# A sparse attention layer: the second part's q is projected in natural row order and gathered from a DRAM table

## The chip, the cores and the metric

The kernel runs on one core of a Trainium2 chip. The metric is the device time of one execution in microseconds (us). The engines are PE (matmul), DVE (vector), ACT (scalar), POOL (GpSimd) and SP; each works through its own instructions in order, and they meet at semaphores. DMAs are issued from SP, ACT and POOL.

## The reference

One graph layer over 4096 nodes with 512 features, 8 heads of 64. `adj` is a symmetric 0/1 matrix with some 17 ones in a row, and a node attends to its neighbours alone. Masks are all ones here. Cut to what is computed:

```python
hs = layer_norm(x, ln1_scale, ln1_bias)
ht = layer_norm(h_target, ln1_scale, ln1_bias)
q = (ht @ Wq + bq).reshape(T, H, HD) / sqrt(HD)
k = (hs @ Wk + bk).reshape(S, H, HD)
v = (hs @ Wv + bv).reshape(S, H, HD)
logits = where(adj != 0, einsum('thd,shd->hts', q, k), NEG)
ctx = einsum('hts,shd->thd', softmax(logits), v).reshape(T, D)
ht = ht + ctx @ Wo + bo
ht = layer_norm(ht, ln2_scale, ln2_bias)
ff = gelu(ht @ W1) @ W2
out = layernorm(x + ht + ff)
```

## The kernel before

The kernel doesn't form the 4096 × 4096 logits. It makes lists of neighbours and gathers only their k and v rows.

**Projections and lists.** `project` norms x, projects k and v, and writes them as rows of 4 KB (k, then v) to the table `kvd` in DRAM. Beside it, `edges` reads the adjacency in quarters of 128 rows × 1024 columns (512 KB each), takes the sign on ACT (L729) with the row's degree as a by-product, and finds the set columns on DVE with MAX8 (L736, five to a quarter) and a few more instructions per tile (L743 to L760). Each row ends as a record: degree (DEG), row number (TGT), row number within its part (ROW), the mean and scale of its first norm (RST), and its neighbours (from E0). The rows are in two parts, 0 to 2047 and 2048 to 4095, of 16 tiles each. `sort` orders a part by degree and scatters its records to DRAM (`recs_d`), so that the rows of one tile have about as many neighbours each; the lists of tile i are CAPS_A or CAPS_B long. Part 0 is sorted before the attention begins; the rest of part 1's lists (`other_lists`) is made beside the attention of part 0.

**Attention.** `attention` goes through the 32 tiles in groups of two (the first and last group have one tile). For a tile, `prefetch` loads its records and `front` makes its q: it gathers the rows of `h_target` by TGT (256 KB), norms them on ACT (L999), turns them with four transposes (L1003), brings them out with scale and bias as four ACT instructions (L1006), projects q with four matmuls (L1012; two records each in the profile), and brings q out on DVE (L1017). The tile `tq` then holds q in its first half and the normed rows, transposed, in its second. L995 is a tie: it makes the norm wait for the newest logits (`latest`). The neighbours come in pieces of S = 3: a piece is three indirect DMAs from POOL (L967), 512 KB each, into a ring of 17 or 20 places; then k times q (L1220) and the sum over each head (L1225) on DVE, the exponential on ACT (L1229, L1238), v times p on DVE (L1184) and ACT (L1204), and on PE the sum over neighbours, as transposes that accumulate in the PSUM tile `cps` (L1192). In the second part DVE first adds two of the three neighbours (L1188).

`finish` ends a tile. It divides by the sum (L1104), puts the normed rows back into natural order with four transposes into the PSUM tile `pa` (L1112), adds ctx @ Wo to them there (L1116), copies the sum to `h` on ACT (L1121), and takes the statistics for the second norm on DVE (L697). A group's normed h goes, transposed, into `h2T`.

**FFN.** `feed` takes a group's `h2T` through W1 (L1325), gelu on ACT (L1328) and W2 (L1334). `end` adds x, norms, and scatters the rows to the output.

**Order.** The streams attention, FFN, `other_lists` and `weights` (late loads of half of W1 and W2) are generators, and `_weave` picks the one with the smallest sum of yielded costs; a group has UNIT = 60 of cost in the attention and as much in the FFN, and `other_lists` starts at WAIT = 40. This gives priorities; a scheduler with a model of its own then fixes each engine's order. Pools hand out buffers in turn by name: `tq` has three, `xt`, `gt`, `h2T` and the PSUM tiles `pf` and `t` have two each.

Of the kernel before, what the change touches and what calls it, by code (L numbers as in the profile page):

```python
# [8 lines left out]
F32 = mybir.dt.float32  # L9
I32 = mybir.dt.int32  # L10
U8 = mybir.dt.uint8
AF = mybir.ActivationFunctionType
ALU = mybir.AluOpType
AX = mybir.AxisListType
# [3 lines left out]
P = 128  # L18
# [425 lines left out]
def adj_resnorm_kernel(  # L444
# [33 lines left out]
    nc = tc.nc  # L478
# [35 lines left out]

    rest_d = dram.tile([N, 2 * SEG * 8], F32, name="rest_d")
# [17 lines left out]
    with tc.tile_pool(name="keep", bufs=1) as keep:  # L533
# [17 lines left out]
        with ExitStack() as late:  # L551
# [157 lines left out]
            def quarter(i, h):  # L709
                if i < RINGED:  # L710
                    a = ring[:, (i * NQ + h) % DEEP, :].bitcast(I32)
                else:
                    a = turn_of("wide", wide)
                nc.sync.dma_start(a, adj[i * P:(i + 1) * P, h * QW:(h + 1) * QW])
                return a

# [247 lines left out]
            recs, tqs, h2Ts, done, ready, latest, newest = {}, {}, {}, set(), [], [], []  # L964

            def gather(dst, table, idx):
                nc.gpsimd.indirect_dma_start(  # L967
                    out=dst, out_offset=None, in_=table[:, :],
                    in_offset=bass.IndirectOffsetOnAxis(ap=idx, axis=0))
# [13 lines left out]
            def front(i, idle=0):  # L983
# [3 lines left out]
                tq = sp.tile([P, 2 * D], F32, name="tq", bufs=3)  # L987
                t = tq[:, :D]
# [89 lines left out]
            def finish(i, p, cps, group, hs, mv):  # L1078
# [31 lines left out]

                for c in range(KC):
                    nc.tensor.matmul(pa[:, c * P:(c + 1) * P], tq[:, D + c * P:D + (c + 1) * P],  # L1112
                                     ident, is_transpose=True, start=c == 0, stop=False,
                                     skip_group_check=True)
                for c in range(KC):
                    nc.tensor.matmul(pa, ct[:, c, :], wo[:, c, :], start=False,  # L1116
                                     stop=c == KC - 1, skip_group_check=True)
# [3 lines left out]
                nc.scalar.copy(h, pa)  # L1121
# [45 lines left out]
            def attention():  # L1167
# [41 lines left out]
                for group in GROUPS:  # L1209
# [3 lines left out]
                    for i in group:  # L1213
                        cps = ps.tile([P, KC, P], F32, name="cps", bufs=2)
                        while k < len(SG) and SG[k][0] == i:
                            _, j0, n = SG[k]
                            while i not in tqs:
# [7 lines left out]
                            nc.vector.tensor_reduce(lg[:, :n, :],  # L1225
                                                    kv[:, :n, :D].rearrange("p j (h d) -> p j h d", h=H),
                                                    AX.X, ALU.add)
# [147 lines left out]

            def chain(gens):
                for g in gens:
                    yield from g
# [65 lines left out]
            def other_lists():  # L1444
                for cost in ed:
# [5 lines left out]
                   (weights(), 0))  # L1451
# [35 lines left out]
```

## Time and profile before

| | us |
|---|---|
| median of 3 runs | 1814.09 |
| lowest, highest | 1813.91, 1817.4 |
| the profiled execution | 1817.49 |
| its span in the profile | 1815.5 |
| first gather of k and v lands, first L1220 | 308.1 |
| first FFN matmul (L1325) | 373.5 |
| scatter of part 1's records (L854) | 627.1 to 664.7 |
| last tile's L1104 | 1706.5 |

The profile gives starts and durations of one execution. Busy times are the union of an engine's instructions. A release is what an idle engine was waiting for. A row of a stretch gives its limits, its length, and for each engine its busy time and number of instructions, then the granted PE clock, the share of the 16 DMA engines, and the GB/s moved.

### The profile page before, as it was taken

How to read it: one execution, taken by the hardware profiler on the slowest of the kernel's cores; microseconds unless marked ns; L12 is line 12 of the kernel's file. 1: busy time of each engine (PE TensorE's matmuls, PEld its weight loads, DVE VectorE, ACT ScalarE, POOL GpSimd, SP SyncE). 2: the span in 40 equal slices, each digit the busy share in tenths (PEclk: the TensorE clock that was granted, in tenths of full speed). 3: DMA queues.
4: the chain of work that ended last, by engine and by line, in shares of the span. 5: the costliest groups of instructions: out<-in, count | busy, mean ns of one | idle time of the engine just before them, and what ended most of it. 6: DMA issues, size and time to landing. Idle time of an engine off the chain costs nothing. (4 is left out here: it accounts for less than half of the span.)

```text
span 1815.5 us, 22973 instructions
## 1 busy us (share of the span) xinstructions
PE 1677.8 (92%) x7030; PEld 1097.9 (60%) x7030; DVE 1436.5 (79%) x2660; ACT 1224.1 (67%) x3121; POOL 982.2 (54%) x834
## 2 busy tenths in 40 slices
PE   7989984597999979999999989999999999999997
PEld 3434442465766656766776757666666666666664
DVE  6989876899999837777978989978878797988200
ACT  5767654487987736766778868877777676787311
POOL 1000144656566676766678788867575665763101
PEclk9999996698999989999999999999999999999998
DMA  9999968989887557777878878787776776774000
GB/s 344 366 380 372 344 198 319 404 287 332 271 305 256 201 173 243 258 255 267 273 263 302 293 260 295 249 285 250 241 266 222 248 251 238 244 248 153 18 6 26
DMA packets 140269, 463.26 MB, mean 255 GB/s; under 512 B 16500, under 2 KB 21672, under 8 KB 140136
## 3 DMA queue, kind: packets, MB, share of 16 engines
q0 software_dynamic: 96656, 342.64, 55.8%
q1 hardware_dynamic: 35664, 95.98, 15.0%
q10 hardware_dynamic: 7816, 23.08, 3.3%
q8 instruction: 58, 0.95, 0.2%
q14 instruction: 75, 0.61, 0.1%
HBM read 430.75 MB, written 30.89 MB: 254 GB/s over the span
## 5 line engine op out<-in xcount | busy, mean ns | idle before, releaser
L967 POOL DMA_INDIRECT kv<-kvd,rec x603 | 758.1, 1257 | 347.5 <-PE cps L1192 139.7
L1334 PE MATMUL po<-w,gt 128*128 128x512 f32 x1024 | 466.4, 598 | 16.2 <-ACT gt L1328 16.2
L1325 PE MATMUL pf<-h2T,w 128*128 128x256 f32 (+1 forms) x2176 | 465.9, 368 | 0.1
L1325 PEld LDWEIGHTS pf<-h2T,w 128*128 128x128 f32 x2176 | 389.3, 191 | 64.5 <-issue 20.3
L1220 DVE TENSOR_TENSOR kv<-kv,tq 128x1536 f32<-128x1536 f32 (+2 forms) x211 | 351.6, 1675 | 68.3 <-DMA kv<-kvd,rec 56.2
L1204 ACT ACTIVATE kv<-kv,pa 128x64 f32<-128x64 f32 x1520 | 391.0, 336 | 4.3
L1225 DVE TENSOR_REDUCE lg<-kv 128x24 f32<-128x1536 f32 (+2 forms) x211 | 350.1, 1666 | 1.4
L1334 PEld LDWEIGHTS po<-w,gt 128*128 128x128 f32 x1024 | 188.8, 192 | 212.4 <-issue 194.3
L1192 PEld LDWEIGHTS cps<-ident,kv 128*128 128x128 f32 x2008 | 240.2, 145 | 109.4 <-issue 59.2
L1192 PE MATMUL cps<-ident,kv 128*128 128x128 f32 x2008 | 264.5, 280 | 44.1 <-DVE kv L1184 24.5
L1184 DVE TENSOR_TENSOR kv<-kv,p 128x1024 f32<-128x1024 f32 (+1 forms) x211 | 251.0, 1193 | 22.8 <-ACT p L1229 20.3
L687 POOL TENSOR_TENSOR n_rs<-n_ve,mhalf 128x2 f32<-128x2 f32 (+2 forms) x51 | 50.8, 997 | 329.1 <-DVE n_ve L680 165.3
L729 ACT ACTIVATE kv<-kv 128x1024 uint8<-128x1024 int32 x128 | 134.9, 1056 | 100.0 <-DMA kv<-in_adj_dram 51.7
L1328 ACT ACTIVATE gt<-pf 128x512 f32<-128x512 f32 x128 | 76.4, 597 | 93.8 <-PE pf L1325 75.8
L1328 ACT ACT_TABLE_LOAD x104 | 133.4, 1283 | 1.7
L736 DVE MAX8 cand<-kv 128x8 uint16<-128x103 uint16 (+1 forms) x640 | 131.8, 252 | 0.8 <-DVE R L755 0.2
L930 PE MATMUL pq<-wk,h2T 128*128 128x512 f32 x256 | 120.8, 616 | 12.1 <-ACT tq L932 7.2
L1012 PE MATMUL t<-wq,tq 128*128 128x512 f32 x256 | 118.2, 605 | 5.6 <-ACT tq L1006 5.6
L930 PE MATMUL pq<-wv,h2T 128*128 128x512 f32 x256 | 115.5, 594 | 6.4 <-ACT kv L729 3.0
L1229 ACT ACTIVATE p<-lg 128x24 f32<-128x24 f32 (+2 forms) x179 | 39.2, 219 | 113.0 <-DVE lg L1225 88.8
L1116 PE MATMUL t<-wo,rb 128*128 128x512 f32 x256 | 115.2, 592 | 0.0
L930 PEld LDWEIGHTS pq<-wk,h2T 128*128 128x128 f32 x256 | 48.9, 197 | 69.9 <-issue 55.2
(160 smaller groups left out, 1582.2 us busy)
## 6 DMA issues: line engine op xcount, KB each, us to landing
kv<-in_adj_dram SPq DMA_DIRECT2D x128, 512.0 KB
kvd<-tq ACTq DMA_DIRECT2D x24, 512.0 KB
kv<-kvd,rec POOLq DMA_INDIRECT x603
kv<-in_L_gnn_h_target_dram SPq DMA_DIRECT2D x32, 256.0 KB
kv<-in_x_dram SPq DMA_DIRECT2D x15, 512.0 KB
rest_d<-gid SPq DMA_DIRECT2D x32, 160.0 KB
w<-in_L_gnn_W_dram SPq DMA_DIRECT2D x4, 1024.0 KB
kvd<-kv ACTq DMA_DIRECT2D x8, 512.0 KB
```

The costliest lines, as they stand in the source:

```text
L729: nc.scalar.activation(sg, a, AF.Sign, accum_out=dpart[:, i, h:h + 1])
L736: nc.vector.max(cand[:, h * SQ + s, :], wd[:, w0:w1])
L930: nc.tensor.matmul(pkv, hT[:, kc, j * P:(j + 1) * P], w[:, kc, :], start=kc == 0, stop=kc == KC - 1)
L967: nc.gpsimd.indirect_dma_start(out=dst, out_offset=None, in_=table[:, :], in_offset=bass.IndirectOffsetOnAxis(ap=idx, axis=0))
L1184: nc.vector.tensor_tensor(v4, v4, p[:, j0:j0 + m, :].unsqueeze(3) .to_broadcast([P, m, H, HD]), ALU.mult)
L1192: nc.tensor.matmul(cps[:, c, :], kv[:, j, D + c * P:D + (c + 1) * P], ident, is_transpose=True, start=j0 + j == 0 and c == 0, stop=j0 + n ...
L1204: newest[:] = [nc.scalar.mul(v, v, pa[:, hd:hd + 1]).ins]
L1220: nc.vector.tensor_tensor(kv[:, :n, :D], kv[:, :n, :D], tq[:, :D].unsqueeze(1).to_broadcast([P, n, D]), ALU.mult)
L1225: nc.vector.tensor_reduce(lg[:, :n, :], kv[:, :n, :D].rearrange("p j (h d) -> p j h d", h=H), AX.X, ALU.add)
L1325: nc.tensor.matmul(pf[:, k, :], w1[(f0 + k) // KC][:, kc, (f0 + k) % KC * P:((f0 + k) % KC + 1) * P], h2T[:, kc, :w], start=kc == 0, stop= ...
L1328: nc.scalar.activation(gt, pf, AF.Gelu_apprx_tanh)
L1334: nc.tensor.matmul(po[j], gt[:, k, j * P:(j + 1) * P], w2[(f0 + k) // KC][:, (f0 + k) % KC, :], start=False, stop=f0 + k == FC - 1, skip_g ...
```

## The change

Part 1's q no longer comes from `front`. A new stream `natural` goes through part 1's 16 tiles of `h_target` in the order of their rows: a load from SP, the norm with the moments that `Rs[1]` holds, four transposes, four ACT instructions with scale and bias, the q projection, four transposes back to natural order, and one row of 4 KB (q, then the normed rows) in the new DRAM table `qd`. It is woven in from the attention's start, at a cost of 5 to a tile. A tile of part 1 then gathers its 512 KB of rows from `qd` by ROW in one indirect DMA, and `finish` adds the normed rows on DVE in place of the transposes and of the ACT copy. Its copy of DEG and TGT to `tags` is issued after the newest logits. Part 0's tiles are as before.

```diff
+    qd = dram.tile([NBT * P, 2 * D], F32, name="qd")
...
+            def behind(ins):
+                return tc.issue_after(ins[-1]) if ins else nullcontext()
...
                 tq = sp.tile([P, 2 * D], F32, name="tq", bufs=3)
+                if TILES[i][0] >= PARTS[1][0] * P:
+                    gather(tq, qd, rec[:, ROW:ROW + 1])
+                    for _ in range(3 + idle):
+                        yield
+                    with behind(logits):
+                        nc.vector.tensor_copy(tags[:, i, :], rec[:, DEG:TGT + 1])
+                    tqs[i] = tq
+                    return
...
+                natural_q = TILES[i][0] >= PARTS[1][0] * P
+                if not natural_q:
+                    for c in range(KC):
+                        nc.tensor.matmul(pa[:, c * P:(c + 1) * P], tq[:, D + c * P:D + (c + 1) * P],
+                                         ident, is_transpose=True, start=c == 0, stop=False,
+                                         skip_group_check=True)
                 for c in range(KC):
-                    nc.tensor.matmul(pa[:, c * P:(c + 1) * P], tq[:, D + c * P:D + (c + 1) * P],
-                                     ident, is_transpose=True, start=c == 0, stop=False,
-                                     skip_group_check=True)
-                for c in range(KC):
-                    nc.tensor.matmul(pa, ct[:, c, :], wo[:, c, :], start=False,
+                    nc.tensor.matmul(pa, ct[:, c, :], wo[:, c, :], start=natural_q and c == 0,
                                      stop=c == KC - 1, skip_group_check=True)
...
-                nc.scalar.copy(h, pa)
+                if natural_q:
+                    nc.vector.tensor_add(h, pa, tq[:, D:])
+                else:
+                    nc.scalar.copy(h, pa)
...
+            def natural():
+                Rf = Rs[1].bitcast(F32)
+                ht, hTs = {}, {}
+                def load(b):
+                    if b < NBT:
+                        ht[b] = sp.tile([P, D], F32, name="xt")
+                        r0 = (PARTS[1][0] + b) * P
+                        nc.sync.dma_start(ht[b], h_target[r0:r0 + P, :])
+                def norm(b):
+                    if b < NBT:
+                        nc.scalar.activation(ht[b], ht[b], AF.Identity,
+                                             bias=Rf[:, b, RST + 1:RST + 2],
+                                             scale=Rf[:, b, RST:RST + 1])
+                def turn(b):
+                    t = ht.pop(b)
+                    pt = ps.tile([P, KC, P], F32, name="t", bufs=2)
+                    for kc in range(KC):
+                        nc.tensor.transpose(pt[:, kc, :], t[:, kc * P:(kc + 1) * P], ident)
+                    hT = sp.tile([P, KC, P], F32, name="gt")
+                    for kc in range(KC):
+                        nc.scalar.activation(hT[:, kc, :], pt[:, kc, :], AF.Identity,
+                                             bias=b1r[:, kc:kc + 1], scale=s1c[:, kc:kc + 1])
+                    hTs[b] = hT
+                def make(b):
+                    hT = hTs.pop(b)
+                    pq = psf.tile([P, D], F32, name="pf")
+                    for kc in range(KC):
+                        nc.tensor.matmul(pq, hT[:, kc, :], wq[:, kc, :], start=kc == 0,
+                                         stop=kc == KC - 1)
+                    pb = psf.tile([P, D], F32, name="pf")
+                    for kc in range(KC):
+                        nc.tensor.transpose(pb[:, kc * P:(kc + 1) * P], hT[:, kc, :], ident)
+                    qn = sp.tile([P, 2 * D], F32, name="h2T")
+                    nc.vector.scalar_tensor_tensor(qn[:, :D], pq, HD ** -0.5, bqr,
+                                                   op0=ALU.mult, op1=ALU.add)
+                    nc.scalar.copy(qn[:, D:], pb)
+                    nc.sync.dma_start(qd[b * P:(b + 1) * P, :], qn)
+                load(0)
+                load(1)
+                norm(0)
+                for b in range(NBT):
+                    turn(b)
+                    load(b + 2)
+                    norm(b + 1)
+                    yield 2.5
+                    make(b)
+                    yield 2.5
...
             _weave((att, 0), (chain(feed(g) for g in range(len(GROUPS))), 0), (other_lists(), WAIT),
-                   (weights(), 0))
+                   (natural(), 0), (weights(), 0))
```

`logits[:]` holds the newest L1225, and `gather` keeps its instruction in `issues`, which nothing reads.

More of the change, by code (lines that the diff above doesn't have):

```diff
@@ L1 @@
-from contextlib import ExitStack
+from contextlib import ExitStack, nullcontext
 import concourse.bass as bass
@@ L964, in adj_resnorm_kernel @@
             recs, tqs, h2Ts, done, ready, latest, newest = {}, {}, {}, set(), [], [], []
+            issues, logits = [], []
             def gather(dst, table, idx):
-                nc.gpsimd.indirect_dma_start(
+                issues[:] = [nc.gpsimd.indirect_dma_start(
                     out=dst, out_offset=None, in_=table[:, :],
-                    in_offset=bass.IndirectOffsetOnAxis(ap=idx, axis=0))
+                    in_offset=bass.IndirectOffsetOnAxis(ap=idx, axis=0)).ins]
             def prefetch(i):
@@ L1224, in attention @@
                             latest[:] = [lg[:, 0, 0:1]]
-                            nc.vector.tensor_reduce(lg[:, :n, :],
-                                                    kv[:, :n, :D].rearrange("p j (h d) -> p j h d", h=H),
-                                                    AX.X, ALU.add)
+                            logits[:] = [nc.vector.tensor_reduce(
+                                lg[:, :n, :], kv[:, :n, :D].rearrange("p j (h d) -> p j h d", h=H),
+                                AX.X, ALU.add).ins]
                             if j0 > 0:
```

## The prediction

> **What bounds the kernel now.** I read the page's engine and slice rows first, then the span cut into stages (busy time by engine in stretches of my choosing), then groups of instructions by form, then the order in which each engine holds its instructions in both kernels.
>
> ```profile
> PE 1677.8 (92%) x7030; PEld 1097.9 (60%) x7030; DVE 1436.5 (79%) x2660; ACT 1224.1 (67%) x3121; POOL 982.2 (54%) x834
> PEclk9999996698999989999999999999999999999998
> DMA  9999968989887557777878878787776776774000
> ```
>
> PE is busy for 92% of the span. The slices with a low clock are those around 270 to 360 us, where PE has the least to do.
>
> ```profile
> core 0: us, PE busy (x) PEld busy (x) DVE busy (x) ACT busy (x) POOL busy (x), PEclk, DMA share, GB/s
> 300.00:373.50 73.50, 37.04 (x171) 27.91 (x170) 61.23 (x82) 34.07 (x119) 51.85 (x42) 0.70 0.98 379
> 373.50:600.00 226.50, 215.28 (x1019) 150.42 (x1019) 219.14 (x471) 182.72 (x458) 133.85 (x113) 0.97 0.85 294
> 600.00:1000.00 400.00, 379.57 (x1776) 266.40 (x1775) 304.78 (x320) 276.48 (x762) 282.75 (x234) 0.98 0.73 247
> 1000.00:1690.00 690.00, 673.87 (x2918) 457.98 (x2917) 595.45 (x694) 514.63 (x1385) 455.20 (x369) 0.99 0.74 246
> 1690.00:1815.50 125.50, 112.56 (x473) 75.11 (x471) 8.38 (x30) 23.53 (x44) 11.29 (x13) 0.96 0.06 18
> ```
>
> The second column is the stretch's length. From 300 to 373.5 (the first gathers, before the first FFN matmul) DMA is full and PE half idle. From 373.5 to 600 DVE is full at 97%: it builds the second part's lists beside the attention. From 1000 to 1690, the second part's tiles, PE is full at 98% and DVE at 86%. After 1690 only PE works on what FFN is left.
>
> ```profile
> L1003 PE MATMUL t<-ident,tq 128*128 128x128 f32 x128 | 21.3, 296 | 12.4 <-ACT tq L999 12.4
> L1012 PE MATMUL t<-wq,tq 128*128 128x512 f32 x256 | 118.2, 605 | 5.6 <-ACT tq L1006 5.6
> L1112 PE MATMUL t<-ident,tq 128*128 128x128 f32 x128 | 19.2, 273 | 0.0
> L999 ACT ACTIVATE tq<-tq,rec 128x512 f32<-128x512 f32 x32 | 25.8, 808 | 7.6 <-DVE rec L995 3.9 <-DMA tq<-in_L_gnn_h_target_dram,rec 3.6
> L1006 ACT ACTIVATE tq<-t,b1r,cols 128x128 f32<-128x128 f32 x128 | 47.8, 457 | 5.7 <-PE t L1003 5.5 <-issue 0.2
> L1017 DVE SCALAR_TENSOR_TENSOR tq<-t,bqr 128x512 f32<-128x512 f32 x32 | 21.6, 675 | 44.7 <-PE t L1012 44.7
> L1121 ACT COPY h<-t 128x512 f32<-128x512 f32 x32 | 18.4, 574 | 32.6 <-PE t L1116 28.9 <-issue 3.7
> ```
>
> These rows hold the moved work, for 32 tiles; 16 tiles move.
>
> **What the Trainium skill says.** "TensorE: Matmul & The Clock Gate", part 1: an idle window of about 3.4 us halves the matmul clock. The trace agrees: 0.70 granted in 300 to 373.5, with PE idle 12.3 us at once. So work put there also raises the clock. "PSUM — Partial Sum Buffer", section on engine and sequencer instructions: ScalarE, VectorE and GpSimd queues are strict FIFO, so an added wait holds all behind it. The trace agrees: ACT sits 12.0 us before an L1201 for one late lg. "DMA: Bandwidth & Descriptors", section on queues: queues share the same 16 engines by turns. In 300 to 373.5 queues 0, 10 and 1 hold 73, 15 and 10% of them, together the 0.98 above, so what SP adds there is taken from the gathers.
>
> **The change part by part.** Counted in both orders, PE, DVE and ACT keep their numbers of instructions; SP gets 32 more. Per engine, for 16 tiles:
>
> PE. Prices at full clock are read from starts in the timeline (start, duration):
>
> ```profile
> 415.01 1.47 PE L1192 MATMUL cps<-ident,kv 128*128 128x128 f32 x12
> 416.32 3.60 PE L1012 MATMUL t<-wq,tq 128*128 128x512 f32 x8
> 419.75 2.78 PE L1192 MATMUL cps<-ident,kv 128*128 128x128 f32 x24
> ```
>
> Twelve transposes hold PE for 1.31 us, 0.109 each, so four take 0.43; a q projection (eight records) takes 3.43. A tile moves 0.43 + 3.43 + 0.43 (L1112, replaced by as many transposes of the normed rows) = 4.29 us; 16 tiles 68.6 us. It leaves the stage where PE is 98% busy and goes to 300 to about 420.
>
> ACT. Norm 0.72, four L1006 1.50, a copy of the normed rows 0.50 (durations less overlap): 2.7 us a tile, 43 us, all early (the first two norms still in the projections, where ACT is 64% busy: free). Later the h copy goes, so the second part loses the same 43 us.
>
> DVE. The q evacuation (0.6 us net) moves early, 10 us. The h add takes the place of the tie (0.22) and that evacuation, so the late stage is as before within 3 us; h now comes to the statistics without the hop over ACT, costed at nothing, since PE sets that stage.
>
> DMA. New loads 16 × 262 KB and writes 16 × 524 KB make 12.6 MB early; late, the gathered row is 4 KB instead of 2 KB, +4.2 MB where DMA has 26% to spare: nothing.
>
> POOL. As many gathers; the tq gather now waits for the DVE add that frees its buffer instead of PE's L1112, with the kv gathers queued behind it. Not shown before; from 0 to 16 × 2 us, taken 8, because the add stands directly behind the wo matmuls that follow L1112 (3.6 us). It is inside the late estimate below.
>
> *Early stage.* In the new order the first FFN matmul comes after 130 cps transposes and the work of natural tiles 0 to 14; before, after 120. So 300 to 373.5 also takes nearly all of the new work, and eight more quarters of the adjacency. DMA: 27.8 MB before + about 11.5 MB of the new + 8 × 0.524 = 43.5 MB; at the 404 GB/s of its saturated slices, 108 us. PE: 27 us at full clock (120 cps transposes at 0.109, 18 records of L1012 and 8 of L1116 at 0.43, 20 other transposes) + 64 = 91. ACT: 34 + 41 + 9 (signs) = 84. DVE: 61 busy + 10 + the list work drawn in, about 85. So DMA sets it: at least 108 us instead of 73.5. SP's loads and writes use pairs of buffers (xt, h2T) and stand in one queue with the adjacency loads, and ACT waits in order for each load, so I take 116: **42 us late**. Bounds: 25 (the extra gathers hide, adjacency not earlier) and 65 (a convoy at 80% of the fullest engine, 135 to 138 us).
>
> *373.5 to 600.* By the 15th attention piece the new order has 543 of the 640 list MAX8, before 485. That is 58 fewer later: 11.6 quarters of 1.2 us (one L734, five L736) and 2.9 tiles of 3.6 us (L743 to L760), 24 us off DVE here. DVE 219 becomes 196, PE 215 + 8 (tiles 14, 15 and their waits) − 5 (430 to 450 ran at a clock of 0.65) = 218. The bound passes from DVE to PE, at 97%: 224 instead of 226.5. Lateness about **40 us** (25 to 62).
>
> *600 to 1000.* PE-bound, same work: 0 ± 5. Nothing catches up.
>
> *1000 to 1690.* A pair of tiles takes 84.0 us (six pairs from 1131.3 to 1635.4), here two of them:
>
> ```profile
> 1300.20:1386.40 86.20, 84.41 (x366) 57.20 (x365) 71.51 (x81) 62.97 (x170) 55.95 (x47) 1.00 0.74 244
> 1465.50:1549.20 83.70, 83.70 (x361) 56.76 (x360) 67.92 (x81) 59.43 (x161) 49.45 (x44) 1.00 0.72 246
> ```
>
> Over the six PE is busy 82.7 a pair and DVE 72.0. Less 8.6, PE needs 75.4 against DVE's 71.8. That near, they don't hide each other fully (373.5 to 600 ran at 97% of the fuller one): 78. So 6 us × 8 pairs, **48 us won**. Bounds: 24 (81 a pair, POOL or DVE stalls) and 68 (all of it).
>
> *Tail.* After the last cps transpose both orders hold the same FFN matmuls: 0.
>
> Sum against the profiled execution: 40 − 48 = −8 us, 1817.5 to 1809.5 (its span is 1815.5). The median of the runs is 1814.09, 3.4 lower, so **1806** is the forecast.
>
> **The rivals.** About 0.2%, 3.6 us, is what a measurement here tells from no change.
>
> Rival A, slower: the early stage becomes a convoy. Place: 305 to 430 us, ACT waiting in order for an h_target load behind an adjacency load on SP, then DVE and PE for ACT. Price: up to 65 us. It decides once the lateness at the first tile of the second part exceeds the late gain, 48. For it: DMA at 0.98, four engines near 85 to 108 us in the same window, buffers in pairs. Against: the gathers run several pieces ahead, and DVE has list work to fill with. At a lateness of 65 and the same late gain: 1814 + 65 − 48 = 1831.
>
> Rival B: the second part doesn't run faster, as DVE (86%) or the gather queue takes over at 81 us a pair. For it: DVE's waits of 21.5 us for POOL's power and 15.6 for p stay. Against: 24.2 of DVE's waits were for the q projection itself, and they go. Won 24, late 40: 1830; with an early stage at its low bound of 25, no change, 1814.
>
> Rival C, a clear gain: the early lateness is at its low bound, 25, and the late gain is 60: 1814 + 25 − 60 = 1779. For it: PE idles 36 us there. Against: DMA's 108 us.
>
> **How the numbers follow.** Forecast case (−4 to −22 us) 0.32; C 0.14; no change 0.12; A 0.27; B's slower end 0.15. Faster 0.46, same 0.12, slower 0.42. The likeliest case alone spans 1792 to 1810. Signs are split, so the range goes from C's middle to somewhat past A: 1778 to 1840.
>
> **What would show it.** The first FFN matmul at 415 ± 10 instead of 373.5, DMA near 400 GB/s until then, the granted clock above 0.9 there; the lists' end at the same attention piece or earlier; then 77 to 80 us a pair in the second part with PE above 95%; the tail still about 115 us. Wrong: the first FFN matmul past 430 with ACT idle before the natural norm or the pb copy (A); pairs still above 81 us with DVE or POOL waiting for each other (B); a first FFN matmul before 400 (C).

## The result, and the profile after

The changed kernel takes 1882.84 us (median; 1878.49 to 1889.95) where the kernel before took 1814.38 in the same comparison (1813.91 to 1817.4): a ratio of 1.0377, 95% interval 1.0341 to 1.0414. It is 68 us slower. The forecast was 1806, with a range to 1840. The profiled execution's span went from 1815.5 to 1883.7 us.

The page's engine rows, the slices of clock and DMA, and the group with the longest idle time on DVE, after:

```profile
PE 1703.3 (90%) x7030; PEld 1102.0 (59%) x7030; DVE 1444.2 (77%) x2660; ACT 1225.3 (65%) x3121; POOL 979.7 (52%) x834
PEclk9999998889899999999999999999999989999998
DMA  9999979978876664867777997888777777775000
L1238 DVE TENSOR_TENSOR kv<-kv,tq 128x1536 f32<-128x1536 f32 (+2 forms) x211 | 352.5, 1677 | 130.3 <-DMA kv<-kvd,rec 114.4
```

TensorE has as many instructions as before and 25 us more of busy time. DVE's first product of a piece (L1238, L1220 before) now waits 130 us (68 before), 114 of them for gathers.

The span after by stages, with the first two cut at the first FFN matmul, which moved from 373.5 to 434.3 us (columns as in the forecast's stage table: length, busy time of PE, PEld, DVE, ACT and POOL, then clock, DMA share, GB/s):

```profile
300.00:373.50 73.50, 55.89 (x207) 31.01 (x206) 50.72 (x76) 39.62 (x122) 30.91 (x27) 0.88 0.96 370
373.50:434.30 60.80, 50.21 (x214) 29.84 (x212) 41.77 (x94) 43.36 (x124) 24.36 (x21) 0.92 0.79 272
434.30:660.80 226.50, 200.75 (x934) 138.18 (x933) 190.97 (x385) 157.13 (x404) 105.45 (x95) 0.96 0.74 252
660.80:1060.00 399.20, 380.20 (x1774) 264.64 (x1773) 296.04 (x314) 263.52 (x724) 273.65 (x231) 0.99 0.72 244
1060.00:1758.00 698.00, 642.00 (x2757) 441.82 (x2757) 605.99 (x694) 504.26 (x1351) 486.23 (x383) 0.96 0.77 258
1758.00:1883.70 125.70, 112.77 (x471) 74.98 (x469) 9.77 (x32) 22.61 (x42) 11.27 (x13) 0.96 0.06 18
```

Three things are to be seen. The first gathers, from 300 us to the first FFN matmul, last 61 us longer, and in them no engine is full (PE 79%; DMA is, at 0.96, for the first 73.5 us alone). From 434 to 661 DVE is no longer full either (it was at 97%). And in the second part PE is busy for 92% of the time where it was at 98%: its work left, and most of the time did not. The stages follow the forecast's round times and don't begin at the same tiles in both kernels, so their lengths are no fine measure.

The finer one is the start of DVE's product that ends a tile (L1104 before, L1117 after), tile by tile. "Late" is how much later than in the kernel before:

| tile | before, us | after, us | late |
|---|---|---|---|
| 1st | 351.2 | 372.0 | 21 |
| 3rd | 414.8 | 487.9 | 73 |
| 7th | 575.2 | 656.8 | 82 |
| 16th, last of the first part | 1032.0 | 1116.5 | 85 |
| 18th | 1131.3 | 1207.6 | 76 |
| 30th | 1635.4 | 1705.2 | 70 |
| 32nd, last | 1706.5 | 1775.2 | 69 |

So the early stage, to the 7th tile, loses 82 us, the rest of the first part 3 more, the second part wins 16, and the tail nothing: 108.5 us follow after the last tile, 109.0 before. The sum is the 68 us of the two spans.

*Early.* The same stretch in both kernels, from 300 us to the seventh tile; first before:

```profile
300.00:575.20 275.20, 227.52 (x1083) 162.08 (x1083) 259.50 (x516) 204.22 (x546) 169.80 (x141) 0.89 0.89 317
```

and after:

```profile
300.00:656.80 356.80, 302.85 (x1330) 195.48 (x1329) 279.46 (x550) 236.24 (x636) 159.86 (x142) 0.94 0.79 279
```

PE's busy time rose by 75.3 us, and its idle time from 47.7 to 54.0 us: in sum, none of the idle time was filled. But they are not the same gaps. PE's main waits in the stretch before (who <- for whom: us in total, times, longest; "issue" is idle time for which the profile shows no wait):

```profile
PE cps L1192 <- DVE kv L1184: 22.7, 4, 12.3
PE cps L1192 <- issue: 11.9, 2, 9.4
```

and some of those after:

```profile
PE cps L1210 <- DVE kv L1202: 6.8, 4, 5.6
...
PE pf L1426 <- ACT gt L1418: 5.5, 2, 2.8
PE t L1415 <- ACT h L1139: 5.4, 1, 5.4
PE t L1415 <- DVE tq L1030: 5.0, 1, 5.0
```

The gaps before the attention's transposes shrank from 34.6 us to 8.2, and new ones of the same size came: 19.4 us before the natural projection's own lines (L1415, L1426, L1430), the rest before other transposes and matmuls. Of the 19.4, 11.8 went by until ACT or DVE had read out the PSUM tile `t`, whose two buffers the natural stream shares with the attention. All engines' waits in the early stage, after (300 to 440 us), the longest that matter:

```profile
POOL kv L972 <- PE cps L1210: 40.8, 11, 10.4
ACT h2T L1434 <- PE pf L1430: 23.4, 7, 10.8
DVE kv L1238 <- DMA kv<-kvd,rec: 14.1, 5, 4.5
ACT xt L1407 <- DMA xt<-in_L_gnn_h_target_dram: 12.3, 5, 5.6
DVE h2T L1432 <- PE pf L1426: 11.8, 5, 6.2
```

This is a convoy: engines that each work in order stand one behind the other. ACT stands before the copy of the normed rows and waits for PE, DVE before the q evacuation for PE, POOL for the ring places that PE's attention transposes (cps) set free, and DVE for the gathers that POOL issues late. PE's timeline in it (start, duration, group):

```profile
319.87 3.60 PE L1426 MATMUL pf<-wq,gt 128*128 128x512 f32 x8
...
338.79 1.97 PE L1210 MATMUL cps<-ident,kv 128*128 128x128 f32 x8 [5.60 <-DVE kv L1202]
340.55 4.15 PE L1426 MATMUL pf<-wq,gt 128*128 128x512 f32 x8
...
348.22 5.40 PE L1426 MATMUL pf<-wq,gt 128*128 128x512 f32 x8
...
358.57 5.40 PE L1426 MATMUL pf<-wq,gt 128*128 128x512 f32 x8 [2.73 <-ACT gt L1418]
```

Between two small groups of attention transposes stands a whole q projection of 3.6 us, and after an idle gap of 5.6 us the same eight records take up to 5.40.

*Late.* Two pairs of tiles of the second part, after:

```profile
1289.30:1372.00 82.70, 77.07 (x325) 53.46 (x324) 74.89 (x85) 58.49 (x156) 65.08 (x51) 0.96 0.82 279
1456.50:1539.20 82.70, 75.81 (x314) 50.99 (x313) 71.84 (x78) 61.39 (x162) 56.27 (x48) 0.94 0.81 272
```

The six pairs from the 18th to the 30th tile take 82.9 us each (84.0 before). PE's busy time fell from 82.7 to 75.7 a pair, and its idle time rose from 1.4 to 7.2. What the engines waited for in these six pairs, after:

```profile
POOL kv L972 <- DVE kv L1206: 38.9, 15, 6.3
DVE kv L1238 <- DMA kv<-kvd,rec: 34.9, 16, 7.8
...
DVE n_nm L693 <- POOL n_rs L688: 20.4, 3, 12.0
...
PE t L1161 <- ACT h L1152: 20.2, 7, 6.8
...
PE cps L1210 <- DVE kv L1206: 8.3, 4, 5.6
```

POOL waits for DVE, DVE for POOL's gathers and for POOL's power, PE for ACT and DVE: a round through four engines, with no engine full. DVE's longest wait for the power, 12.0 us at 1267.3, was for 0.74 us of work: between DVE's request at 1253.0 and the power at 1266.5 POOL ran ten gathers that stood before it.

### The profile page after: what moved, and what is told of

The parts are those of the page before. It is cut to its first block, busy times and chain, and to the rows that moved or that the text cites. A ratio compares the mean times of both kernels' runs of the same rounds, so it can differ in the third digit from the quotient of the medians.

```text
span 1883.7 us, 23025 instructions
## 1 busy us (share of the span) xinstructions
PE 1703.3 (90%) x7030; PEld 1102.0 (59%) x7030; DVE 1444.2 (77%) x2660; ACT 1225.3 (65%) x3121; POOL 979.7 (52%) x834
## 5 line engine op out<-in xcount | busy, mean ns | idle before, releaser
L972 POOL DMA_INDIRECT kv<-kvd,rec x603 | 749.7, 1243 | 391.4 <-PE cps L1210 160.2
L1352 PE MATMUL po<-w,gt 128*128 128x512 f32 x1024 | 473.8, 605 | 22.9 <-ACT gt L1346 22.9
L1238 DVE TENSOR_TENSOR kv<-kv,tq 128x1536 f32<-128x1536 f32 (+2 forms) x211 | 352.5, 1677 | 130.3 <-DMA kv<-kvd,rec 114.4
L1210 PEld LDWEIGHTS cps<-ident,kv 128*128 128x128 f32 x2008 | 234.6, 143 | 98.3 <-issue 40.8
L1346 ACT ACTIVATE gt<-pf 128x512 f32<-128x512 f32 x128 | 76.4, 596 | 90.1 <-PE pf L1343 86.7
```

The source lines that it names most:

```text
L972: issues[:] = [nc.gpsimd.indirect_dma_start(out=dst, out_offset=None, in_=table[:, :], in_offset=bass.IndirectOffsetOnAxis(ap=idx, axis=0) ...
L1210: nc.tensor.matmul(cps[:, c, :], kv[:, j, D + c * P:D + (c + 1) * P], ident, is_transpose=True, start=j0 + j == 0 and c == 0, stop=j0 + n ...
L1238: nc.vector.tensor_tensor(kv[:, :n, :D], kv[:, :n, :D], tq[:, :D].unsqueeze(1).to_broadcast([P, n, D]), ALU.mult)
L1346: nc.scalar.activation(gt, pf, AF.Gelu_apprx_tanh)
L1352: nc.tensor.matmul(po[j], gt[:, k, j * P:(j + 1) * P], w2[(f0 + k) // KC][:, (f0 + k) % KC, :], start=False, stop=f0 + k == FC - 1, skip_g ...
```

## The experiments

Eighteen kernels were run, all in comparison with the kernel before. "Late at 7th" is the lateness of the seventh tile, "won" how much that lateness fell from the 16th tile to the last, "pair" the mean of the six pairs; all are from the profiled execution of each.

Two cautions. The executions of one kernel differ by up to 17 us (e13: 1804.91 to 1821.89 in 20 runs), and a profile is one of them: e9's is the fastest of its 17, e15's the slowest of its 7. So a microsecond a pair says little by itself. And the scheduler fixes each engine's order anew for each kernel, so an edit can do more than leave something out. Counting successive matmuls of one line and tile as one group, PE's order is that of the changed kernel in e1 from the 16th tile to the last (282 of 282 groups; DVE's and ACT's orders too), and in e2 and e3 up to the 7th tile (172 of 172). It is partly another one in e5 (141 of e2's 173 groups stand in the same sequence) and in e11 (256 of e1's 282, among 330). In e13 and e14 it is that of the kernel before from the 22nd tile on (194 of 194), but of DVE's 407 instructions there only 354 and 361 keep their sequence.

| run | ratio to before, 95% interval | late at 7th | won in the second part | pair |
|---|---|---|---|---|
| the changed kernel | 1.0377 (1.0341 to 1.0414) | 82 | 16 | 82.9 |
| e1_late_alone | 0.9945 (0.9927 to 0.9964) | 3 | 13 | 83.3 |
| e2_early_alone | 1.0459 (1.0425 to 1.0492) | 85 | 0 | 84.0 |
| e3_no_dma | 1.0308 (1.0285 to 1.0332) | 68 | 15 | 83.2 |
| e4_after_lists | 1.0386 (1.0354 to 1.0417) | 2 | 14 | 83.0 |
| e5_quarter_q | 1.0229 (1.0190 to 1.0269) | 42 | 1 | 83.9 |
| e6_late_no_hop | 1.0072 (1.0054 to 1.0091) | 20 | 8 | 84.4 |
| e7_late_balance | 1.0143 (1.0102 to 1.0183) | 21 | -8 | 86.4 |
| e8_before_no_hop | 1.0109 (1.0069 to 1.0149) | 18 | -7 | 84.7 |
| e9_third_on_sp | 0.9973 (0.9960 to 0.9987) | -4 | 12 | 83.1 |
| e10_no_add | 1.0014 (0.9998 to 1.0030) | -2 | 2 | 84.8 |
| e11_less_wo | 0.9705 (0.9687 to 0.9722) | -5 | 53 | 77.7 |
| e12_less_act | 0.9915 (0.9882 to 0.9947) | -4 | 20 | 82.3 |
| e13_before_less_q | 0.9965 (0.9951 to 0.9979) | 3 | 4 | 82.9 |
| e14_before_less_wo | 0.9768 (0.9743 to 0.9792) | -1 | 37 | 79.0 |
| e15_late_nm | 0.9940 (0.9917 to 0.9963) | 3 | 10 | 83.8 |
| e16_late_turn | 0.9966 (0.9937 to 0.9996) | 2 | 14 | 83.5 |
| e17_late_no_power | 0.9901 (0.9868 to 0.9935) | 4 | 23 | 81.6 |
| e18_before_no_power | 0.9956 (0.9944 to 0.9968) | 0 | 7 | 83.0 |

### The two halves of the change by themselves

**e1_late_alone** keeps the second part of the changed kernel and one natural tile:

```diff
-                for b in range(NBT):
+                for b in range(1):
...
-                    gather(tq, qd, rec[:, ROW:ROW + 1])
+                    gather(tq, qd, Rs[1][:, 0, ROW:ROW + 1])
```

> Leaves out the natural projection but for one tile of 16; all second-part tiles gather their q and normed rows from that one tile's 128 rows, with the same number and size of gathers as after. The early stage should then be as before (first FFN matmul near 378 instead of 434), and the second part shows what the table wins by itself. Theory 1 (the table wins 6 us a pair as forecast, and the changed kernel's 83 us a pair come from being thrown out of step early): pairs of 77 to 79 us and 1765 to 1775 in all. Theory 2 (without the q projection the second part is held by the round of gather, logits, exponentials, values and transposes, which PE's freed time does not shorten): pairs of 82 to 83 us, first tile of the second part as before, and 1797 to 1805 in all.

**e2_early_alone** keeps the natural projection, and lets the second part work as before:

```diff
-                if TILES[i][0] >= PARTS[1][0] * P:
+                if False:
                     gather(tq, qd, rec[:, ROW:ROW + 1])
...
-                natural_q = TILES[i][0] >= PARTS[1][0] * P
+                natural_q = False
```

> Does the natural projection as after and writes the table, but the second part projects its own q from gathered rows as before, so the table is not read. The early cost alone. Theory 2 (early cost of 84 us at the seventh tile stays, second part at its old 84 us a pair): 1895 to 1905. Theory 1: the same early cost. If the early cost were caught up later because PE then is the bound everywhere: 1880 or less.

Measured: 1809.14 us for the first (its comparison's before: 1817.82), 1904.0 for the second. In e1 the first FFN matmul is back at 374.5, and the pairs are 81.8, 82.7, 84.3, 83.6, 79.9 and 87.6: those of the changed kernel, 81.7, 82.6, 84.5, 82.7, 80.9 and 85.1. So the early delay does not spoil the second part; the table wins 13 us there by itself, near what theory 2 expected or a little less. In e2 the seventh tile is 85 us late and stays 86 to 88 late to the end. The spans add up within 11 us: -7.3 and +86.7 give +79.4, where the whole change has +68.2; e1 still holds a natural tile, some 5 us of lateness.

### What the early stage pays for

**e3_no_dma** takes 14 of the 16 loads and 15 of the 16 writes away, by the count of bytes 11.5 of the 12.6 MB (not 12, as expected below), and leaves the instructions of PE, ACT and DVE:

```diff
-                    if b < NBT:
-                        ht[b] = sp.tile([P, D], F32, name="xt")
+                    if 2 <= b < NBT:
+                        ht[b] = two[b % 2]
+                    elif b < NBT:
+                        ht[b] = two[b] = sp.tile([P, D], F32, name="xt")
...
-                    nc.sync.dma_start(qd[b * P:(b + 1) * P, :], qn)
+                    if b == 0:
+                        nc.sync.dma_start(qd[b * P:(b + 1) * P, :], qn)
```

> After, with natural's DMAs left out except for the first two loads and one write: the later tiles norm the same two rows of tiles again and their results are not written, and the second part gathers from the one written tile. PE, ACT and DVE instructions are the same as after, 12 of the 12.6 MB are not moved. If the early cost is DMA's bytes in a full stage: 12 MB at 404 GB/s are 30 us, so the first FFN matmul near 404 and about 1853 in all. If it is the in-order chain PE, ACT, PE, DVE laid between the attention's pieces (a convoy of engines, the loads only a part of it): the first FFN matmul at 420 or later and 1868 to 1883. If ACT's waits for loads were most of it: the first FFN matmul at 395 or earlier and under 1845.

**e5_quarter_q** is e2 with one of four q matmuls a natural tile:

```diff
-                    for kc in range(KC):
-                        nc.tensor.matmul(pq, hT[:, kc, :], wq[:, kc, :], start=kc == 0,
-                                         stop=kc == KC - 1)
+                    nc.tensor.matmul(pq, hT[:, 0, :], wq[:, 0, :], start=True, stop=True)
```

> e2_early_alone (natural projection early, table written but not read), with only one of the four q matmuls of each natural tile: the other three, 2.57 us of TensorE a tile by the starts in the trace, 41 us in all, are left out; every other instruction and every DMA stays. If the early cost is TensorE work standing in order before the attention's transposes, and counted nearly one for one: 87 us late falls to 46 to 52, 1863 to 1869 in all. If it is the waits of natural's chain between PE, ACT and DVE (a convoy whose length the matmuls don't set): still 70 or more late, 1885 to 1900.

**e4_after_lists** sets the natural projection behind the second part's lists, in places of the ring that the lists have left (two for the loads, but one each for the turned rows and the result, where the changed kernel has two):

```diff
                 yield from sort(1)
+                yield from natural()
...
-                    yield 2.5
+                    yield 3.5
```

> After, with natural moved from the first gathers to behind the second part's lists (tiles 10 to 14 of the first part), in buffers that the lists no longer use. There DMA has a quarter to spare and DVE a quarter, but PE is 95% busy. If the early cost is the collision in the first gathers and moved PE work is otherwise only moved: lateness 0 until tile 9, then 60 to 68 us of PE work less what its 5% of idle time takes in, 50 to 65, at the first tile of the second part, less 15 won in the second part: 1850 to 1865. If natural's chain is itself the trouble wherever it stands: 80 or more late there, 1875 to 1890.

Measured. e3: 1872.79 us, the first FFN matmul at 422.6, the seventh tile 68 late. Its stretch from 300 us to the seventh tile:

```profile
300.00:643.50 343.50, 302.55 (x1338) 195.73 (x1337) 281.52 (x554) 234.87 (x636) 159.47 (x145) 0.94 0.75 261
```

PE's busy time is that of the changed kernel (302.85), its idle time 41 us instead of 54. So nearly all of the natural DMAs together cost 13 of the 82 us. e5: 1857.42 us; 41 us of matmuls left out bring the seventh tile from 85 to 42 us late, and the first FFN matmul from 437.9 to 410.7:

```profile
300.00:617.60 317.60, 263.44 (x1251) 179.92 (x1250) 269.50 (x524) 236.18 (x634) 168.20 (x141) 0.92 0.87 313
```

PE's busy time is 44.8 us less than in e2 (308.28), the stretch 42.9 us shorter, its idle time 54.2: PE's work there counts about one for one (a little more than was expected; part of the order changed too), and 41 to 54 us of idle time stand beside it with 0, 36 or 75 us of added work. As shown above these are not the same gaps each time: the added work closes some and opens others. That the engines' waits for each other set their sum is read from the waits; no run took such a wait away by itself, for instance by giving the natural stream a `t` of its own.

e4: 1886.14 us. The first gathers are as before (seventh tile 2 us late), and between the 10th and the 14th tile the lateness grows from 3 to 82 us, not to 50 to 65. The stretches are, nearly to the tile, before,

```profile
725.50:913.20 187.70, 184.42 (x861) 129.13 (x860) 151.67 (x160) 134.50 (x369) 127.45 (x110) 0.99 0.78 262
```

and in e4

```profile
727.80:995.20 267.40, 258.65 (x1132) 169.20 (x1131) 163.20 (x179) 176.72 (x469) 120.62 (x110) 0.99 0.67 231
```

79.7 us longer for 74.2 us of PE's busy time. The moved work costs as much where PE is full as it did in the first gathers, where PE was half idle. With PE at 98% there was next to nothing to hide it under, so e4 does not tell whether the collision in the first gathers made it dear there; it shows that this later place is no cheaper.

### Why the second part wins so little

The next four look for an engine that took over from PE. e6 moves one small product behind the power from DVE to POOL, in both parts (a sign change stays on DVE, ahead of the power); e7 also drops every second DVE add of value rows in favour of four transposes; e8 is e6's edit in the kernel before.

```diff
+                ng = sp.tile([P, 2], F32, name="n2_ng")
+                nc.vector.tensor_scalar_mul(ng[:, :nh], mv[:, :nh, 0], -1.0)
...
-                nm = negmean(sp, mv[:, :nh, :], rs, nh, "n2")
+                nm = sp.tile([P, nh], F32, name="n2_nm")
+                nc.gpsimd.tensor_tensor(nm, ng[:, :nh], rs, ALU.mult)
...
-                if m > 1 and i >= NA:
+                if m > 1 and i >= NA and j0 // S % 2:
```

> e1_late_alone (one natural tile, second part reads the table), with the small product behind the second norm's power moved from DVE to POOL, so that DVE, which works in order, no longer waits for POOL there (20.4 us in six pairs of the changed kernel, up to 12 at once). If DVE's in-order time, busy 71.5 us and idle 11 of a pair's 83, now sets the second part: pairs of 79 to 80.5 us and 1778 to 1792 in all. If the gathers' round through POOL and the ring sets it: pairs still 82 to 83 and 1800 to 1810, with DVE's idle time put down to the gathers instead.

> e6_late_no_hop, and every second piece of the second part without its DVE add of two value rows (0.6 us net each, about 6.4 a pair): TensorE transposes the second row into the sum instead (0.43 us each). A pair has 3.8 us less of DVE and 2.8 us more of PE. If DVE sets the second part: pairs of 76 to 77.5, 25 us less than e6_late_no_hop. If PE at 91% is already what sets it: pairs longer than in e6_late_no_hop by 2 to 3 us. If POOL's gathers set it: no change.

> The kernel before with the edit of e6_late_no_hop alone. There PE is 98% busy in the second part, so DVE's wait for POOL (17.2 us in six pairs) should cost nothing: 1810 to 1818, pairs at 84 us. A gain of 10 us or more would say that PE was not the bound of the kernel before, and that the late term of the forecast was wrong from its start.

Measured: 1828.82, 1844.06 and 1836.64 us. The edit of e6 was a bad probe: it takes DVE's wait away and puts ACT behind POOL's gathers. In e6 from 1207 to 1640 us, some five of its pairs:

```profile
ACT h L1155 <- POOL n_nm L1153: 39.6, 6, 16.9
...
PE t L1164 <- ACT h L1155: 29.7, 9, 14.1
```

It also cost 17 to 18 us by the 7th tile, with the table and without, so e6 and e8, which met none of their expectations, tell nothing of the bound. e7 against e6 does: 4.2 us a pair less busy time on DVE and 3.3 more on PE made the pair 2.0 us longer. Less work on DVE does not help, and PE's time counts for the most part, though PE is busy for 90 to 92% of the pair only.

e9 to e12 each take one engine's work away from e1:

```diff
+                    if i >= NA and j == 2:
+                        nc.sync.dma_start(kvs[k][:, j, :], kvd[1 + i * P:1 + i * P + P, :])
...
-                        nc.vector.tensor_add(kv[:, 0, D:], kv[:, 0, D:], kv[:, 1, D:])
...
-                for c in range(KC):
+                for c in range(KC - 1 if natural_q else 0, KC):
                     nc.tensor.matmul(pa, ct[:, c, :], wo[:, c, :],
...
-                    for hd in range(H):
+                    for hd in range(H if k < first_b else 2):
```

> e1_late_alone, in which one gather of three in each piece of the second part is replaced by a plain load of 128 rows on SP's queue: the same bytes, but some 13 gathers a pair less in POOL's queue (1.24 us each, 16 us a pair), and the third row no longer has to wait behind POOL's other work. It leaves out the third neighbour of each piece (fixed rows are taken). If POOL's queue (busy 60 of 83 us, idle for the ring and for issue in the rest) sets the second part now: pairs of 75 to 79 us and 1750 to 1775 in all. If DMA's bytes or the ring's space set it: 82 to 84. If PE or DVE in their order set it: 81 to 83.

> e1_late_alone without the DVE add of two value rows in the second part (its second row is left out of the sum): 13 adds of 0.6 us net, 7.8 us of DVE a pair less, nothing else changed. If DVE in its order sets the pair: 76 to 78 us a pair, about 1765. If POOL's queue sets it: 82 to 84, no change.

> e1_late_alone with one of the four output-projection matmuls a tile in the second part (three left out): 2.57 us of TensorE a tile, 5.1 a pair. If PE (75.7 of 83 us busy) still sets the pair: 78 to 79 us. If, as after the first 8.6 us, its time is no longer what counts: 82 to 83.5.

> e1_late_alone with two of the eight ScalarE products of the third value row in each piece of the second part (six left out, 0.34 us each, 2 us a piece, 26 us a pair). ACT is busy 58 of 83 us, but it stands in order between DVE's logits and DVE's products. If ACT's place in the round sets the pair: 78 us or less. If not: 82 to 83.5.

Measured: 1811.08, 1817.5, 1762.9 and 1800.09 us. A third of POOL's gathers less: pair 83.1 for 83.3, though the first pair fell to 69.0 and the fourth to sixth rose to 89; by the medians the kernel is no faster. DVE's add left out: no gain (84.8). Three quarters of ACT's products of the third value row left out, 26 us a pair as a sum of durations and 17 of ACT's busy time: 1 us. Only e11 was worth its size: PE's busy time fell by 6.0 us a pair, and the pair by 5.6. Two of its pairs:

```profile
1207.60:1284.50 76.90, 72.58 (x317) 49.82 (x317) 72.39 (x81) 59.55 (x155) 57.49 (x48) 0.98 0.82 281
1434.10:1510.90 76.80, 73.12 (x325) 51.72 (x324) 69.92 (x80) 62.64 (x166) 59.88 (x45) 0.98 0.84 284
```

DVE holds 70 to 72 us of work a pair here and the pair is 77; so neither DVE nor POOL held e1 at 83 by its amount of work. That was the explanation I had (rival B), and it falls with this run.

Two questions were left: does the table's own new work eat the gain, or was the q projection free where it stood? **e13** and **e14** leave the table out, and take three of four matmuls from one place or the other of the kernel before:

```diff
-                for kc in range(KC):
-                    nc.tensor.matmul(pq, hT[:, kc, :], wq[:, kc, :], start=kc == 0,
+                k0 = KC - 1 if i >= NA else 0
+                for kc in range(k0, KC):
+                    nc.tensor.matmul(pq, hT[:, kc, :], wq[:, kc, :], start=kc == k0,
...
+                    if i >= NA and c < KC - 1:
+                        continue
                     nc.tensor.matmul(pa, ct[:, c, :], wo[:, c, :], start=False,
```

> The kernel before with one of the four q matmuls a tile in the second part (three left out): 2.57 us of TensorE a tile, 5.1 a pair, as e11_less_wo takes from the output projection, but no table. If the table's own new work (the gather that waits for DVE's add, the add itself, the tags) eats the gain of the freed TensorE time: pairs of 78 to 80 us here, 1772 to 1785. If the q projection's TensorE time was free in its place, because it stood where TensorE would otherwise wait for the second norm: pairs of 82 to 83.5, 1800 to 1812.

> The kernel before with one of the four output-projection matmuls a tile in the second part, TensorE's order and the q projection otherwise as they are. If TensorE's total time sets the second part of the kernel before: 5 us a pair, pairs of 78.5 to 80 and 1770 to 1780. If only places in the chain from the values to the second norm count, the same; if neither, 83 and 1805 or more. With e13 it tells a total from a place.

Measured: 1813.77 and 1777.72 us, against 1819.05. The same 41 us of TensorE work win 4 us in the second part when they are q matmuls and 37 when they are output-projection matmuls. From the 22nd tile to the last, where PE's groups stand in the same order in all three, the kernel before takes 406.3 us, e13 399.1 and e14 379.1. One pair of e13 (85.4, where its six are 82.9 on average),

```profile
1218.80:1304.20 85.40, 78.88 (x339) 53.30 (x340) 76.72 (x87) 65.65 (x170) 65.79 (x53) 0.98 0.83 276
```

and one of e14:

```profile
1443.30:1521.30 78.00, 78.00 (x348) 54.16 (x348) 67.86 (x81) 59.46 (x161) 55.86 (x44) 1.00 0.78 264
```

In its six pairs PE stays full in e14 and does not in e13; its waits for DVE's adds there, which don't occur in the six pairs of the kernel before, are in e13

```profile
PE cps L1193 <- DVE kv L1189: 11.9, 6, 4.9
```

and in e14

```profile
PE cps L1194 <- DVE kv L1190: 3.6, 3, 1.8
```

So the table is not needed to explain the small gain: q time in the second part was nearly free before it was touched, though PE showed itself 98% busy. A full engine is not one number; what its time is worth depends on the place in its order. How much of the difference is due to DVE's order, which the scheduler changed a little in both, was not told apart.

The last four ask which wait became bare. e15 sets the second norm's product, e16 only its transposes, two steps later; e17 and e18 take POOL's power out of the second part's second norm, with the table and without (a reciprocal stands for the power -0.5).

```diff
                 rs = power(sp, mv[:, :nh, :], nh, "n2", ve)
                 yield
+                if natural_q:
+                    yield
+                    yield
...
                 w = len(hs) * P
...
+                if i >= NA:
+                    rs = sp.tile([P, nh], F32, name="n2_rs")
+                    nc.vector.reciprocal(rs, ve)
```

> e1_late_alone with the second norm's product (DVE, waiting for POOL's power) and all behind it two steps, one piece, later in the order of the second part. If TensorE and DVE wait there because the q projection that covered this chain is gone: the 20 us of each go, pairs of 79 to 80.5, less a tail some 6 us longer: 1785 to 1797. If the waits only move to the next place: pairs of 82.5 to 84, 1808 to 1820.

> e1_late_alone with only the transposes of the second norm's rows (TensorE, waiting for ACT's norm) two steps later in the second part, the norm itself where it was. If TensorE's wait for ACT there (20.2 us in six pairs) is what the pair pays: pairs of 80 to 81, 1790 to 1800. If DVE's wait for POOL is: no change, 83.

> e1_late_alone, in the second part with a reciprocal on DVE where the second norm takes the power -0.5 on POOL (the square root is left out). DVE no longer waits for POOL there, and POOL's gathers for the pieces ahead no longer stand behind an instruction that waits for DVE, ACT and the output projection. If this round (output projection, DVE's statistics, POOL's power in its queue of gathers, DVE) is what holds the second part, and so why freed q time does not count there and freed output-projection time does: DVE's waits for POOL (20 us in six pairs) and for gathers (37 us) mostly go, pairs of 77 to 80, 1765 to 1790. If not: pairs of 82 to 84, 1803 to 1815.

> The same edit in the kernel before. If TensorE's time is the bound there and the round lies just below it: within 1 us a pair, 1808 to 1820. If the round already set the second part of the kernel before, with TensorE's 98% busy only filling it: 3 us a pair or more, below 1795.

Measured: 1810.7, 1809.98, 1797.35 and 1809.32 us. Moving the norm's chain later wins nothing: in e16 PE's wait for ACT's norm goes (from 9.4 us in e1 to 1.5), and its wait for DVE's add grows, from 7.9, most of it in one wait:

```profile
PE cps L1213 <- DVE kv L1209: 18.1, 2, 12.3
PE po L1355 <- ACT gt L1349: 12.4, 5, 4.9
```

Without POOL's power e17 takes 1.7 us a pair off e1, where 3 to 6 were expected. DVE still waits for gathers and POOL for DVE (1130 to 1630 us):

```profile
DVE kv L1242 <- DMA kv<-kvd,rec: 44.5, 22, 7.4
...
POOL kv L972 <- DVE kv L1210: 48.7, 20, 6.2
```

In the kernel before the same edit wins 1.0 us a pair. By the ratios to the kernel before it wins 8 us in both: from 0.9945 to 0.9901 with the table, from 1 to 0.9956 without. So POOL's power was a little on the path with PE full as well, and that it got worse with the table is not shown.

Not settled: which wait makes the q projection's place free and the output projection's dear. The runs exclude POOL's number of gathers, DVE's add, most of ACT's products and the place of the second norm as the one cause. POOL's power costs a little, but about as much without the table, so that it explains the missing 7 us a pair is not shown.

## Why the prediction was wrong

The forecast was 77 us too low: 44.5 of them in the first part (84.5 us late, not 40), and 32 in the second (16 us won, not 48).

**The bytes were right, the overlap was not.** Forecast were 43.5 MB until the first FFN matmul; moved were 370 GB/s for 73.5 us and 272 for 60.8, 43.7 MB. At 404 GB/s that is the 108 us of the forecast; it took 134.3. The step that failed is "So DMA sets it: at least 108 us instead of 73.5". It takes the fullest resource for the length of the stage, and so hides PE's 64 us of moved work under DMA's 108. What the runs show in its place: nearly all of the natural bytes cost 13 us (e3), and 41 us of the moved matmuls cost 43 (e5). The sum that fits is the simplest: 16 tiles by 4.3 us of PE, about 69, of which nothing is hidden, plus 13 for the DMA: 82, as measured; for e5 it gives 69 - 41 + 13 = 41 where 42 was measured. It was found after the result, on one kernel.

**"PE idles 36 us there" was read as cover.** 22.7 us of those gaps, before, ended on DVE's value products, which the attention transposes wait for. PE works in order, so a q projection of 3.6 us set between attention transposes delays these, then the ring's places, then the gathers and DVE, and PE waits elsewhere. The forecast cited the section on engine and sequencer instructions of "PSUM — Partial Sum Buffer" in the Trainium skill for the strict queues of ScalarE, VectorE and GpSimd; the same section has matmuls start and complete in program order, and PE's timeline agrees: the projection at 319.87 us stands whole before the next attention transposes, at 323.85. The clock did rise (0.70 to 0.88 and 0.92), nearly as expected, and does not show in the sum.

**373.5 to 600.** Forecast: 40 late at the end of it, since 24 us of list work drawn ahead would come off DVE. The lists did finish at the same tile, their scatter between the eighth and the ninth in both (709 to 746 us after, 627 to 664 before), but the lateness rose from 61 at the first FFN matmul to 82 at the seventh tile. What the list work drawn ahead may have won does not show.

**600 to 1000 and the tail.** 0 ± 5 and 0 were forecast; +3 (a lateness of 82, then 85) and 0 were measured.

**1000 to 1690.** Here "PE needs 75.4 against DVE's 71.8" came out at 75.7 and 71.5, PE's by luck: 75.4 is the pair's length, 84.0, less 8.6; PE's busy time of 82.7 less 8.6 is 74.1, and 7.0 of the 8.6 left. The step that failed is "That near, they don't hide each other fully ...: 78. So 6 us × 8 pairs, 48 us won": 82.9 a pair, 13 to 16 won. The allowance was taken from a stage where DVE was full and PE at 95%; it held no measure of what waits appear once no engine is. It also took each microsecond of a 98% busy PE for worth a microsecond; e13 shows 4 us from 41 for this work, and why is the question left open above.

**The tq gather's wait** behind DVE's add, taken at 8 us, was 7.1 in the six pairs; in e1's six pairs no idle time of DVE stands before the h add (12 of 0.68 us), and neither DVE nor ACT waits for it. So the waits were as small as thought; what they cost in time was not measured by itself.

**The rivals.** A's signs came (a first FFN matmul past 430, ACT idle before the pb copy 23.4 us and before the natural norm 12.3), and so did B's (pairs above 81, DVE and POOL waiting for each other). They were priced each against the forecast's other half, 1831 and 1830; both together were not a case; with the measured sizes together they are 1814 + 82 - 16 = 1880. A's convoy is there, but not by its trigger, loads behind adjacency loads on SP: without nearly all natural loads and writes (e3) 68 of the 82 us stay. B's mechanism, that DVE or the gather queue takes over as the bound, is not what the runs show. A's price of at most 65 was exceeded since the lateness, 61 at the first FFN matmul, went on growing after it.

## What to carry to other kernels

Before work is moved, leave it out where it stands: two runs, each with three of four matmuls gone at one place, showed that 41 us of a 98% busy engine were worth 4 us in one place and 37 in the other. See then whether the order changed with it. And idle time of an in-order engine that waits for others is not simply cover for work placed between the waiting instructions: here 75 us of it closed some gaps and opened as many. Count moved work at its full length until a run shows otherwise.

## What the hardware showed unexpectedly

After PE's idle gap of 5.6 us eight attention transposes took 1.97 us instead of 1.04, and the following q projections 4.15 to 5.40 us instead of 3.60: the moved work was dearer for the waits around it. The Trainium skill, "TensorE: Matmul & The Clock Gate", part 1, has the clock halved after an idle window of about 3.4 us, and the trace agrees for this gap: 0.50 was granted from 334.8 to 341.6 us. It was granted again from 348.5 to 351.9 and from 358.7 to 362.1, where the longest gaps just before were 1.2 and 2.7 us. In the second part the clock was 0.94 to 1.00 by pairs, with 7 us of PE's idle time in each (1.00 over the six pairs before), and of 8.6 us of work taken out only 7.0 left PE's busy time; that the one made the other fits, but was not tried by itself. A gather's stay on POOL was not constant: 0.94 us for most, up to 4.26 us in e1's second part, and taking a third of them off POOL's queue (e9) did not make the kernel faster: 1811.08 us against 1809.14.
